# A Mamba layer and a mixture-of-experts block on one core: power, routing, transfers, projection and final sums rearranged

## The chip, the core and the metric

The kernel runs on one core of a Trainium2 chip. Five engines work side by side, each through its own queue in order: TensorE (PE) multiplies matrices into PSUM, VectorE (DVE) does element-wise work, statistics and scans, ScalarE (ACT) applies functions with a scale and a bias, GpSimd (POOL) does small element-wise work and issues the indirect transfers, SyncE (SP) issues most of the plain transfers. The metric is the time of the device in microseconds, as the median of several runs.

## The reference

Two layers over 4 sequences of 1024 tokens with 128 features, in float32.

```python
# layer 1: Mamba, then LayerNorm of x + layer
xb, z = split(x @ in_proj_w.T)                  # 256 channels each
xb = silu(conv4(xb)); dt_in, Bp, Cp = split(xb @ x_proj_w.T)
dt = softplus(dt_in * dt_w + dt_b); A = -exp(A_log)
h[t] = exp(dt*A) * h[t-1] + (xb*dt) * Bp[t]     # 16 states for each channel
y = (h * Cp).sum(states) + xb * D
x = layernorm(x + (norm(y) * ln_g + ln_b) * silu(z) @ out_w.T)
# layer 2: attention, then 16 experts of which each token takes two
hidden = x + causal_attention(norm(x), 16 heads of 8) @ o_w
xt = norm(hidden); logits = xt @ router_w
top1, top2 = two largest of softmax(logits), with a limit of 512 rows per expert
eout[e] = gelu(rows_of_e @ fc1_w[e]) @ fc2_w[e] * 0.8
moe = g1 * eout[top1] + g2 * eout[top2]
x = layernorm(x + hidden + moe)
```

A token's row stands in its expert's list at the count of earlier tokens with the same choice, so routing needs running counts over all tokens.

## The kernel before

The tokens are 32 tiles of 128, a sequence is 8 tiles, a half of a sequence is 4. Everything lies in one program with two branches; the one that runs is the one under `with tc.If(mild > 0)`.

**Stage 1, scans.** `fronts` makes the projections and the convolution. `scans` then takes the halves of the sequences one after the other; the scans proper are VectorE instructions over 512 tokens (L511), with the exponentials from ScalarE (L505) and products on both sides (L501, L517), and the sums over states on TensorE (L521). After the scans of a half, `after_scans` norms y and projects it: it makes y centred on TensorE (`pt_yc`, L449), multiplies it into the gate on VectorE (`sz`) and squares it on ScalarE (`sq`), sums the squares on TensorE into the variances (`pv`, L469), takes their power -0.5, and projects the gated rows (`pa`). `on_half` then norms the rows twice (`lnx`) and `inputs` of the attention makes queries and keys from them (`xh`, `pt_xn`, `pq`), which go out to DRAM (`q_parts`, `k_parts`) and come back spread (`qst`, `kst`).

**Stage 2, attention.** `stream` goes through blocks of 128 keys against 512 queries: scores on TensorE (L742), exponentials on ScalarE (L752), weighted sums on TensorE (L764). When the four groups of heads of a half are done, `rest_of_half` (or `group_of_last` for the very last half) divides, projects, and `after_projection` adds, norms (`hid` to `xrow`, with `normalise_in_pieces`), transposes (`pt_x2`) and makes the router's logits (`lg`).

**The order.** From the second sequence on, TensorE and VectorE run in the order in which the program is written (`manual_schedule`, engines in `pinned`); for the other engines a scheduler chooses. The streams of work are Python generators that `piece` advances in turn: `before` (what leads to the next inputs: `after_scans`, `inputs`), `after` and `final` (what follows attention), `aside` (the routing of tiles that are ready), `loads` (the experts' weights) and `sending` (row transfers). A piece contains one step of the attention (`next(attend)`). A generator that yields `USE` has its next part put ahead of the attention's block, others behind. `pace.first` holds from the end of the scans on: then `before` gets an extra step.

**Routing.** `routing` gives `send(t0, n, later)`: the two largest logits for n tiles, running counts by products with a triangle and with ones on TensorE (`pcum`), the slot of each row (`put`), and then one indirect transfer for each tile and choice (`scatter`, line L126) from `xrow` to the experts' lists `xin` in DRAM. It is called three times, for 20, 8 and 4 tiles. The transfers of the first call carry no group, and so each waits until the one before it has landed; from the second call on they are declared independent of each other.

**Powers.** `inv_std` adds epsilon on VectorE and takes the power on GpSimd, for all norms (L152).

**Stage 3, experts.** For each of 16 experts: rows read from `xin`, transposed, multiplied (`ph`), GELU on ScalarE (`hT`), multiplied (`po_e`), bias added (`eo`), and written by four indirect transfers to `eout`, at the place of the token. `all_sent` computes the final gates after the third expert.

**Final sums.** For each four tiles both choices' rows are read (`got0`, `got1`), multiplied by the gates and added to the residual rows `x1` on VectorE (L1446), normed (`lno`) and written out.

Of the kernel before, what the change touches and what calls it, by code (L numbers as in the profile page):

```python
# [10 lines left out]
F32 = mybir.dt.float32  # L11
BF16 = mybir.dt.bfloat16
I32 = mybir.dt.int32
AF = mybir.ActivationFunctionType
# [5 lines left out]
P = 128  # L20
B, L, D = 4, 1024, 128
T = B * L
# [30 lines left out]
def mamba_then_moe_block_kernel(ctx: ExitStack, tc: tile.TileContext, a: dict, out: bass.AP):  # L53
# [43 lines left out]
    pace = Step(slack=False, hold=False, first=False, block=False, quiet=0)  # L97

    def slack():
        if pace.slack:  # L100
            yield
# [52 lines left out]

    def normalise(*args):
        for _ in normalise_in_pieces(*args):
            pass

    def normalise_in_pieces(pool, src, dst, n, tag):

        mv = statistics(pool, src, n, tag)
        r = inv_std(pool, mv[:, :, 1], n, tag)
        yield USE
        apply_norm(src, dst, mv, r, n)
# [174 lines left out]
    def scans(ph, pools, on_loads, on_scans, on_half, spare_bank=lambda: None):  # L339
# [99 lines left out]
        def after_scans(b, hf, y, sz, r):  # L439
# [26 lines left out]
            pv = bank("pv")  # L466
            for i in range(TPH):
                for c in range(NC2):
                    nc.tensor.matmul(  # L469
                        pv[:, i : i + 1], lhsT=sqs[c][:, i * P : (i + 1) * P], rhs=mean_col,  # L470
                        start=(c == 0), stop=(c == NC2 - 1),
                    )
            yield USE
            rs = inv_std(n2, pv[:, 0:TPH], TPH, "ssm")
            yield
            pa = project("pa", sz, w_out)
            yield from slack()
            yield USE
# [137 lines left out]
    def attention(ph, weights, last_bank):  # L616
# [235 lines left out]
        def group_of_last(e, g, t, rows, i0, n):  # L852
# [28 lines left out]
            if g < NG - 1:  # L881
                yield
# [6 lines left out]
            if g == NG - 1:  # L889
                pace.quiet += 1  # L890
                yield USE
                yield from after_projection(e, po, rows, i0, n, e.hid if i0 else None)

        def tokens_of_half(e, po, rows):
            if pace.first:
                pace.quiet += 1
            poT = p1.tile([P, 512], F32, tag="poT", name="poT")
            nc.scalar.activation(poT, po, AF.Identity, bias=ob)
            yield
            pt = bank_z("pt_po")  # L900
            for i in range(4):
                nc.tensor.transpose(pt[:, i * P : (i + 1) * P], poT[:, i * P : (i + 1) * P], ident)
            yield from slack()
            yield USE
            yield from after_projection(e, pt, rows, 0, TPH)

        def after_projection(e, pt, rows, i0, n, hid=None):
# [18 lines left out]
            if pace.quiet:  # L926
                pace.quiet -= 1
# [238 lines left out]
    def routing(ph, bank):  # L1166
# [51 lines left out]
        def send(t0, n, later=None):  # L1218
# [14 lines left out]

            group = (f"sent{t0}", []) if t0 or later is None else None
            earlier = sent[-1] if sent else []
            if group:
                sent.append(group[1])

            def transfers(i):
                for t in range(t0, t0 + n):  # L1240
                    ins = scatter(xin, put[i][:, t : t + 1], xrow[:, t, :], group, earlier)
                    if group and (len(group[1]) == 1 or earlier):
                        wait_for(ins, earlier)
                    yield
# [70 lines left out]
            if later is not None:  # L1315
                yield
# [67 lines left out]
    def experts(ph, weights, behind, sent, all_sent):  # L1384
# [4 lines left out]
        p4 = ph.enter_context(tc.tile_pool(name="moe4", bufs=4))  # L1389
        ps_t = ph.enter_context(tc.tile_pool(name="ps_t", bufs=2, space=PSUM))  # L1390
# [42 lines left out]


        x1 = p1.tile([P, NT, D], F32, tag="x1", name="x1")
        nc.sync.dma_start(x1, rest_d.rearrange("(i p) d -> p i d", p=P))
        for t0 in range(0, NT, 4):
            s = p3.tile([P, 4, D], F32, tag="s", name="s")
            for k in range(2):
                r = p3.tile([P, 4, D], F32, tag=f"got{k}", name=f"got{k}")  # L1440
                read = (nc.sync, nc.scalar)[k].dma_start(
                    r, eout[k * T + t0 * P : k * T + (t0 + 4) * P, :].rearrange("(i p) d -> p i d", p=P)
                )
                wait_for(read.ins, made[1])
                for i in range(4):
                    nc.vector.scalar_tensor_tensor(  # L1446
                        s[:, i, :], r[:, i, :], gates[k][:, t0 + i : t0 + i + 1],
                        x1[:, t0 + i, :] if k == 0 else s[:, i, :], ALU.mult, ALU.add,
                    )
            o = p3.tile([P, 4, D], F32, tag="o", name="o")  # L1450
            normalise(p3, s, o, 4, "lno")
            nc.sync.dma_start(out[t0 * P : (t0 + 4) * P, :].rearrange("(i p) d -> p i d", p=P), o)
# [6 lines left out]
    with tc.If(mild > 0) as cmp:  # L1459

        with ExitStack() as late:
            with ExitStack() as ph:
# [8 lines left out]
                def piece():  # L1471

                    pace.block = False
                    for at in (USE, None):
                        for s in (late_loads, before, after, final, aside, loads, sending):
                            if at is None:
                                pause = middle and not pace.block
                                if s is after and pace.hold or s is before and pace.first:
                                    continue
                                if s is loads and (before or pause) or s is sending and (pace.quiet or pause):  # L1480
                                    continue
# [75 lines left out]
                xrow, send, all_sent, (behind, sent), rows.tri = routing(late, lambda name: (last_bank if before else bank)(name))  # L1557
# [23 lines left out]
            experts(late, moe_w, behind, sent, lambda: all_sent(early))  # L1581
    with cmp.Else():
# [21 lines left out]
        with ExitStack() as late:  # L1604
# [7 lines left out]
            experts(late, moe_w, behind, sent, lambda: all_sent(NT // 2))  # L1612
# [67 lines left out]
```

## Time and profile before

| | |
|---|---|
| time before, median of 3 runs | 1277.02 us (1276.29 to 1282.18) |
| the profiled execution | 1282.12 us, its span 1280.3 us |
| TensorE busy | 934.2 us, 73% of the span |
| VectorE busy | 890.2 us, 70% |
| ScalarE busy | 644.3 us, 50% |
| GpSimd busy | 247.9 us, 19% |
| mean granted TensorE clock | 0.813 |
| last scan starts | 859.8 us |
| first read of the experts' rows is issued | 1077.1 us |
| first read of the final sums is issued | 1229.1 us |

In lines of the timeline the columns are the start and the duration in us, the engine, the line of the kernel, the operation, the tiles (out<-in) with shapes, the number of instructions merged, and in brackets how long the engine stood idle before and which instruction ended that. In the table of stages each engine's busy time is followed by its number of instructions; PEclk is the granted TensorE clock, 1.0 being full speed. A wait is put down to what came last by the profile. `L` numbers are lines of the kernel before. The profiled execution was at the upper end of the runs.

### The profile page before, as it was taken

The numbers are of one execution on the slowest core, as the hardware profiler recorded it, in microseconds if no ns is written. First come the engines' busy times: TensorE is split into PE (matmuls) and PEld (weight loads), VectorE is DVE, ScalarE is ACT, GpSimd is POOL, SyncE is SP. The second block draws the span as 40 slices with busy tenths as digits, with TensorE's granted clock in tenths as the row PEclk, the third lists the DMA queues.
The fourth block names the chain that finished last, engine by engine and source line by source line (L and its number), as shares of the span: only waits on it lengthen the run. The fifth ranks groups of instructions, "written<-read, shape, count | busy, mean of one in ns | idle before, by whom it ended". The sixth has DMA issues, their size and how long they took to land. (4 is left out here: it accounts for less than half of the span.)

```text
span 1280.3 us, 14950 instructions
## 1 busy us (share of the span) xinstructions
PE 934.2 (73%) x5248; PEld 428.1 (33%) x5248; DVE 890.2 (70%) x1319; ACT 644.3 (50%) x900; POOL 247.9 (19%) x225
## 2 busy tenths in 40 slices
PE   4687851358798988799887599878759863998910
PEld 2232310035333334234333233334313322665610
DVE  2299698998998987988999998896324433212146
ACT  1467556334876775477774278753333621332300
POOL 0020121022102001011003120101232342344421
PEclk9988975557998889689888679889676865999965
DMA  3965576426545433552552441243543115122042
GB/s 72 335 232 174 195 260 230 161 99 193 176 127 167 148 120 121 152 154 91 167 178 90 155 131 38 84 119 84 168 137 96 35 34 184 60 66 65 29 131 84
DMA packets 168311, 170.99 MB, mean 134 GB/s; under 512 B 31537, under 2 KB 123138, under 8 KB 168098
## 3 DMA queue, kind: packets, MB, share of 16 engines
q1 hardware_dynamic: 150818, 142.11, 35.9%
q10 hardware_dynamic: 13312, 19.40, 4.3%
q0 software_dynamic: 4096, 8.43, 1.9%
q8 instruction: 43, 0.70, 0.2%
q14 instruction: 42, 0.34, 0.1%
HBM read 110.80 MB, written 59.10 MB: 133 GB/s over the span
## 5 line engine op out<-in xcount | busy, mean ns | idle before, releaser
L752 ACT ACTIVATE pr<-pst 128x1024 f32<-128x1024 f32 (+3 forms) x396 | 293.2, 792 | 122.8 <-PE pst L742 61.1
L505 ACT ACTIVATE da<-dt_sp,a_neg 128x512 f32<-128x512 f32 x256 | 179.1, 721 | 111.9 <-DVE h L511 101.5
L742 PE MATMUL pst<-qst,kst 72*128 72x512 bf16 (+3 forms) x792 | 205.6, 363 | 36.2 <-ACT pr L752 26.7
L764 PE MATMUL av<-pr,vp 128*32 128x512 f32 (+3 forms) x1584 | 192.4, 554 | 4.5 <-DVE pr L755 2.6
L511 DVE TENSOR_TENSOR_SCAN h<-da,carry,h 128x512 f32<-128x512 f32 x128 | 156.0, 1268 | 1.7 <-ACT da L505 1.7
L501 DVE TENSOR_TENSOR h<-u_sp,bt 128x2048 f32<-128x2048 f32 x64 | 145.4, 2276 | 16.0 <-DMA u_sp<-u_d 16.0
L511 DVE TENSOR_TENSOR_SCAN h<-da,h 128x512 f32<-128x512 f32 x128 | 148.7, 1207 | 6.6 <-ACT da L505 6.6
L517 DVE TENSOR_TENSOR h<-h,ct 128x2048 f32<-128x2048 f32 x64 | 146.3, 2285 | 1.1 <-POOL carry L514 0.3
L521 PE MATMUL py<-h,sel 128*32 128x512 f32 x512 | 87.3, 762 | 81.3 <-DVE h L517 53.7
L742 PEld LDWEIGHTS <-kst 72*128 72x128 bf16 x792 | 68.2, 106 | 186.9 <-issue 170.6
L514 POOL COPY carry<-h 128x4 f32<-128x4 f32 x32 | 40.0, 1249 | 353.1 <-DVE h L511 353.1
L1412 ACT ACTIVATE hT<-ph,b 128x512 f32<-128x512 f32 x64 | 43.9, 687 | 89.4 <-PE ph L1411 87.8
L126 POOL DMA_INDIRECT xin<-xrow,put x64 | 63.6, 994 | 104.5 <-DMA xin<-xrow,put 87.5
L126 POOL DMA_INDIRECT eout<-eo,to x64 | 61.5, 960 | 91.0 <-DVE eo L1423 55.7
L1411 PE MATMUL ph<-xeT,w 128*128 128x512 f32 x128 | 64.3, 639 | 12.9 <-DVE xeT L1407 12.9
L281 PE MATMUL pt_x<-xT,w_tap 128*128 128x512 f32 x128 | 60.6, 629 | 17.5 <-DVE w_tap L263 7.4
L1418 PEld LDWEIGHTS po_e<-w,hT 128*128 128x128 f32 x512 | 61.5, 192 | 13.2 <-issue 12.7
L748 PE MATMUL pst<-mask_k,identb 128*128 128x128 bf16 x448 | 63.9, 227 | 0.0
L1418 PE MATMUL po_e<-w,hT 128*128 128x128 f32 x512 | 63.2, 277 | 0.1
L764 PEld LDWEIGHTS av<-pr,vp 128*32 128x32 f32 x1584 | 36.9, 114 | 65.2 <-issue 39.7
L748 PEld LDWEIGHTS <-identb 128*128 128x128 bf16 x448 | 43.7, 103 | 26.7 <-issue 7.6
L521 PEld LDWEIGHTS py<-h,sel 128*32 128x32 f32 x512 | 12.1, 120 | 120.1 <-DVE h L517 66.8
(231 smaller groups left out, 1098.4 us busy)
## 6 DMA issues: line engine op xcount, KB each, us to landing
dt_sp<-dt_d SPq DMA_DIRECT2D x64, 256.0 KB
u_sp<-u_d SPq DMA_DIRECT2D x64, 256.0 KB
kst<-k_parts SPq DMA_DIRECT2D x96, 144.0 KB
qst<-q_parts SPq DMA_DIRECT2D x64, 144.0 KB
bt<-bc_d SPq DMA_DIRECT2D x32, 256.0 KB
ct<-bc_d SPq DMA_DIRECT2D x32, 256.0 KB
w<-in_fc_w_dram SPq DMA_DIRECT2D x32, 256.0 KB
xin<-clear SPq DMA_DIRECT2D x8, 516.0 KB
```

Source lines behind the costliest of these rows:

```text
L126: ins = nc.gpsimd.indirect_dma_start(out=dst[:, :], out_offset=bass.IndirectOffsetOnAxis(ap=rows, axis=0), in_=src, in_offset=None).ins
L501: nc.vector.tensor_tensor(s.h, s.u, four(s.bt), ALU.mult)
L505: nc.scalar.activation(s.da[jl], s.dt[:, jl, :], AF.Exp, scale=a_neg[:, j, s.g : s.g + 1])
L511: ins = nc.vector.tensor_tensor_scan(h, s.da[jl], h, from_, ALU.mult, ALU.add).ins
L517: nc.vector.tensor_tensor(s.h, s.h, four(s.ct), ALU.mult)
L521: nc.tensor.matmul(s.py[jl * NR : (jl + 1) * NR, :], lhsT=sel, rhs=s.h[:, jl, :], start=(s.g == 0), stop=(s.g == NG_S - 1),)
L742: nc.tensor.matmul(pst[:, jj, :w], lhsT=ks[ki // TPH][jp][:, jj, ki % TPH * P : (ki % TPH + 1) * P], rhs=qs[jp][:, jj, q0:c1], start=True, ...
L748: nc.tensor.matmul(pst[:, jj, :P], lhsT=identb, rhs=mask_k, start=False, stop=True)
L752: nc.scalar.activation(pr[:, :, :w], pst[:, :, :w], AF.Exp, scale=QSCALE)
L764: nc.tensor.matmul(av[32 * j : 32 * j + 32, q0 : q0 + w], lhsT=e.vps[ki // TPH][:, ki % TPH, v0 : v0 + 32], rhs=pr[:, jj, :w], start=(ki = ...
L1411: nc.tensor.matmul(phh, lhsT=w1[e][:, c * P : (c + 1) * P], rhs=xeT, start=True, stop=True)
L1418: nc.tensor.matmul(po[:, i, :], lhsT=hT[:, c, i * P : (i + 1) * P], rhs=w2[e][:, c, :], start=(c == 0), stop=(c == NFC - 1),)
```

## The change

1. *No power on GpSimd without scans*: where `pace.first` holds, `normalise_in_pieces` takes the power by three Newton steps on VectorE, 14 instructions, and no longer yields in between.
2. *Projection with the variances*: where a second PSUM bank is free (`spare_bank`), `after_scans` writes `pv` there and issues `pa` right behind it; the rest of the half before is held meanwhile (`pace.hold`).
3. *Routing behind inputs*: `aside` and the transfers advance only when `before` is empty; transfers and loads only with an attention block. The counter `quiet`, which held transfers off while a power was due, goes. The routing's bank is the common one.
4. *Transfers not in turn*: the first call's transfers get a group too. After the first choice's transfers the routing yields `USE`.
5. *Final sums by TensorE*: each gate is put on a diagonal by ScalarE (`by_gate`), during the experts in the source; two products per tile add both choices in PSUM. The residual rows are read into `xrow` after the third expert. ScalarE norms by scale and bias. Both choices lie in one tile, five deep. The last group is two groups of two tiles.

```diff
+    def inv_std_steps(pool, var, n, tag):
+        ve = pool.tile([P, n], F32, tag=tag + "_ve", name=tag + "_ve")
+        nc.vector.tensor_scalar(ve, var, LN_EPS, None, ALU.add)
+        r = pool.tile([P, n], F32, tag=tag + "_rs", name=tag + "_rs")
+        t = pool.tile([P, n], F32, tag=tag + "_nt", name=tag + "_nt")
+        nc.vector.tensor_scalar(r.bitcast(I32), ve.bitcast(I32), 1, None, ALU.logical_shift_right)
+        nc.vector.tensor_scalar(r.bitcast(I32), r.bitcast(I32), -1.0, float(0x5F3759DF), ALU.mult, ALU.add)
+        for _ in range(3):
+            nc.vector.tensor_tensor(t, r, r, ALU.mult)
+            nc.vector.tensor_tensor(t, t, ve, ALU.mult)
+            nc.vector.tensor_scalar(t, t, -0.5, 1.5, ALU.mult, ALU.add)
+            nc.vector.tensor_tensor(r, r, t, ALU.mult)
+        return r
...
-        r = inv_std(pool, mv[:, :, 1], n, tag)
-        yield USE
+        if pace.first:
+            r = inv_std_steps(pool, mv[:, :, 1], n, tag)
+        else:
+            r = inv_std(pool, mv[:, :, 1], n, tag)
+            yield USE
...
-            pv = bank("pv")
+            other = spare_bank()
+            pv = (other or bank)("pv")
...
+            if other:
+                pace.hold = True
+                pa = project("pa", sz, w_out)
+                yield from slack()
             yield USE
             rs = inv_std(n2, pv[:, 0:TPH], TPH, "ssm")
-            yield
-            pa = project("pa", sz, w_out)
-            yield from slack()
-            yield USE
+            pace.hold = False
+            if other:
+                yield USE
+            else:
+                yield
+                pa = project("pa", sz, w_out)
+                yield from slack()
+                yield USE
...
-            if g < NG - 1:
+            if not i0:
                 yield
             po = zbank("po") if i0 else e.po
...
-            group = (f"sent{t0}", []) if t0 or later is None else None
+            group = (f"sent{t0}", [])
             earlier = sent[-1] if sent else []
-            if group:
-                sent.append(group[1])
+            sent.append(group[1])
...
             if later is not None:
-                yield
+                yield USE
...
+                nc.sync.dma_start(xrow[:, :, 0:D], rest_d.rearrange("(i p) d -> p i d", p=P))
+                by_gate = p6.tile([P, NT, 2, P], F32, tag="by_gate", name="by_gate")
+            elif e > 2:
+                per = -(-NT // (E - 3))
+                for t in range((e - 3) * per, min((e - 2) * per, NT)):
+                    for k in range(2):
+                        nc.scalar.activation(
+                            by_gate[:, t, k, :], ident, AF.Identity, scale=gates[k][:, t : t + 1]
+                        )
...
-        x1 = p1.tile([P, NT, D], F32, tag="x1", name="x1")
-        nc.sync.dma_start(x1, rest_d.rearrange("(i p) d -> p i d", p=P))
...
-                    nc.vector.scalar_tensor_tensor(
-                        s[:, i, :], r[:, i, :], gates[k][:, t0 + i : t0 + i + 1],
-                        x1[:, t0 + i, :] if k == 0 else s[:, i, :], ALU.mult, ALU.add,
...
+        for t0, n in [(t, 4) for t in range(0, NT - 4, 4)] + [(NT - 4, 2), (NT - 2, 2)]:
+            both = ps_h.tile([P, CAP], F32, tag="ph", name="both")
+            for i in range(n):
+                for k in range(2):
+                    nc.tensor.matmul(
+                        both[:, i * D : (i + 1) * D], lhsT=by_gate[:, t0 + i, k, :], rhs=gots[t0 + i][:, k, :],
+                        start=(k == 0), stop=(k == 1),
+                    )
+            s = p3.tile([P, 4, D], F32, tag="s", name="s")[:, :n, :]
+            nc.vector.tensor_tensor(
+                s, both[:, : n * D].rearrange("p (i d) -> p i d", d=D), xrow[:, t0 : t0 + n, 0:D], ALU.add
+            )
+            mv = statistics(p3, s, n, f"lno{n}")
+            nm = p3.tile([P, 4], F32, tag="lno_nm", name="lno_nm")[:, :n]
+            nc.vector.tensor_scalar(nm, mv[:, :, 0], -1.0, None, ALU.mult)
+            r = inv_std(p3, mv[:, :, 1], n, f"lno{n}")
+            sh = p3.tile([P, 4], F32, tag="lno_sh", name="lno_sh")[:, :n]
+            nc.gpsimd.tensor_tensor(sh, nm, r, ALU.mult)
+            o = p3.tile([P, 4, D], F32, tag="o", name="o")[:, :n, :]
+            for i in range(n):
+                nc.scalar.activation(
+                    o[:, i, :], s[:, i, :], AF.Identity, bias=sh[:, i : i + 1], scale=r[:, i : i + 1]
+                )
...
-                                pause = middle and not pace.block
                                 if s is after and pace.hold or s is before and pace.first:
                                     continue
-                                if s is loads and (before or pause) or s is sending and (pace.quiet or pause):
+
+                                if s is aside and before or (s is loads or s is sending) and (before or middle and not pace.block):
                                     continue
...
-                xrow, send, all_sent, (behind, sent), rows.tri = routing(late, lambda name: (last_bank if before else bank)(name))
+                xrow, send, all_sent, (behind, sent), rows.tri = routing(late, bank)
```

## The prediction

> **What bounds the kernel now.** I first read the table of stages (busy time of each engine in stretches of the span), because this program runs through four stages with different limits, then the waits of VectorE, then the timeline around the two longest stalls, and last the chain that ended last.
>
> ```profile
> core 0: us, PE busy (x) PEld busy (x) DVE busy (x) ACT busy (x) POOL busy (x), PEclk, DMA share, GB/s
> 300.00:400.00 100.00, 87.76 (x651) 41.97 (x653) 87.86 (x109) 69.99 (x104) 15.13 (x8) 0.95 0.50 158
> 950.00:1000.00 50.00, 40.22 (x178) 13.56 (x182) 18.02 (x58) 17.06 (x23) 17.29 (x18) 0.58 0.23 71
> 1240.00:1280.30 40.30, 0.00 (x0) 0.00 (x0) 28.27 (x139) 0.00 (x0) 7.12 (x7) 0.50 0.37 103
> ```
>
> With scans (to about 862 us) VectorE and TensorE are both at 88%. Without scans (862 to 1060) VectorE is at 36%, and TensorE, at a granted clock of 0.58, carries the time. In the last 40 us TensorE and ScalarE do nothing and VectorE runs alone with GpSimd.
>
> The waits of VectorE with scans, 100 to 862 us (total, times, longest):
>
> ```profile
> DVE ssm_ve L150 <- PE pv L469: 13.6, 7, 3.5
> DVE xh L176 <- POOL lnx_rs L490: 9.2, 6, 1.5
> DVE x L480 <- PE pa L425: 2.6, 3, 1.1
> ```
>
> Seven times VectorE stands still for the variances of the centred rows, 1.9 us each.
>
> The timeline without scans, for the longest stall:
>
> ```profile
> 944.21 0.17 DVE L150 TENSOR_SCALAR ln_ve<-ln_mv 128x4 f32<-128x4 f32 x1
> 956.44 1.07 POOL L152 TENSOR_TENSOR ln_rs<-ln_ve,neg_half 128x4 f32<-128x4 f32 x1
> 957.94 1.25 PE L936 MATMUL pt_x<-ident,xrow 128*128 128x128 f32 x4 [10.39 <-DVE xrow L176]
> ```
>
> The variance is ready at 944.4, but its power starts at 956.4: GpSimd's queue stood in row transfers, each waiting for the one before it. The list of all waits has POOL xin behind DMA xin at 87.5 us in 41 waits. TensorE was idle for 10.39 us.
>
> The inputs of the last half of a sequence, TensorE's lines of the same timeline:
>
> ```profile
> 893.86 1.38 PE L645 MATMUL pt_xn<-ident,xh 128*128 128x128 f32 x4 [5.15 <-DVE xh L176]
> 907.57 2.07 PE L661 MATMUL pq<-xnT,wk 128*128 128x512 f32 x2 [2.61 <-DVE rest L667]
> 915.83 1.01 PE L742 MATMUL pst<-qst,kst 72*128 72x512 bf16 x2 [2.51 <-DMA qst<-q_parts]
> ```
>
> From the last y at 865.8 to the first score at 915.83 it takes 50 us, with TensorE waiting on VectorE, which meanwhile routes 20 token tiles.
>
> The chain that ended last, in the final sums:
>
> ```profile
> 1263.71 1.11 DVE o L176 x4
> 1264.83 1.31 DVE s L1446 x5
> 1266.14 0.40 DVE lno_st L170 x2
> 1267.13 0.24 DVE s L1446
> 1267.92 1.02 POOL lno_rs L152
> ```
>
> One group of four tiles every 5.25 us, on VectorE, with a wait of 0.94 us for the power.
>
> **What the Trainium skill says.** (1) "TensorE: Matmul & The Clock Gate", section "HAM oscillation — how this bites in real kernels", warns of idle gaps over about 3.4 us, after which TensorE's clock halves. The trace agrees as to the fall (clock 0.50 from 945 to 982) but not as to recovery: from 958 TensorE was busy, and it stayed at 0.50 until about 982. (2) "DMA: Bandwidth & Descriptors", section "Anatomy of one DMA — SWDGE (gpsimd) path", gives a nearly fixed 2 us, most of it the receipt of the write. Here 0.96 us of issue and at least 1.6 us of wait: 2.5 us and more for each transfer in turn, against 1.27 us start to start where they don't wait (1023 to 1036). (3) "SBUF — State Buffer", section "Who interferes with whom", has GpSimd and VectorE block each other on a shared port pair. The power of 128x4 took 1.01 us while VectorE was quiet and 1.85 to 3.00 among scans.
>
> **The change, part by part.** The sum is made on the profiled execution: span 1280.3, 1.8 us around it, 1282.1.
>
> Final sums. Removed from VectorE: per group 8 multiply-adds (8 x 0.26 us start to start) and 4 normalisations (1.11 us). There remain one add from PSUM (0.69, the row of eo, same shape), statistics of 4 tiles (1.16, the 1.40 of the trace less the 0.24 of a multiply-add between them) and two small ones (0.24): 2.1 us; for seven groups of four and two of two some 17.2 us. TensorE gets 64 products, two passes each: 128 x 0.12 us (26 passes of po_e took 3.1), at half clock 0.215 (eight passes of ph took 6.62 against 3.70). The first 6.6 us of the experts after idling were at half clock, so I take 7 us for two groups, then 95 x 0.12 = 11.4: 18.4 us, beside VectorE. ScalarE takes the four normalisations, some 0.31 us each (row probs, 128x128), 1.2 us a group: hidden. GpSimd gets a second small product per group, which no row shows quiet: between 0.3 and 1.25 us (the carry copy among scans); I take 0.6, so 2.2 us a group with the hand-overs, just about VectorE's pace. Transfers: 4 MB in and 2 MB out at the 300 GB/s seen at 1231 to 1235 need 21 us, also about that pace. First data 1233.5 (as now, k=1), first sums 1236.9, VectorE done 1254.1, then power, product and normalisation of two tiles (1.9) and the 5.3 us from the last row to the end as now: 1261.3. The gain is 19 us; 10.7 if TensorE stays at half clock (128 x 0.215 = 27.5), 12.8 if GpSimd sets 2.8 us a group, 21 at best. The read of the residual rows (2 MB, now at 1060.7 in the wait for the last transfers) moves into the third expert, on SP ahead of the fourth expert's rows; there the queue sat waiting for buffers, so nothing.
>
> Gates on diagonals: 64 ScalarE instructions. In the order of the changed program 30 stand ahead of the first GELU. The gates are ready at 1070.1, 30 x 0.31 = 9.3 us end at 1079.4, and the table load before the first GELU came at 1084.18: hidden. 14 follow the first expert (4.3 us in the 5.9 us of idle ahead of the second): hidden. Of 20 around the second expert's GELUs, 6 us, the third expert's GELUs (1103.1) are late by some 3: I charge 2.5, with ends 0 and 6.
>
> Power on VectorE without scans: 14 dependent steps of 128x4 or 128x2 at 0.21 us (the routing's steps of 128x20 follow each other so, 889.5 to 890.4) are 2.9 us, in place of 1.0 on GpSimd. At the stall: from the transposed projection 0.15 + 0.72 + 1.73 + 0.12 + 2.9 + 0.33 = 6.0 us to the first row, less 2 to 3 us of TensorE work between: TensorE waits 3.7 in place of 10.4, and its wait of 2.2 us just before (on a masked tile behind those statistics) goes: gain 8.5. The last norm lies on the path: 1.9 more. The one before it meets a projection put one block later, which saves some of the 3.41 us TensorE waited at 1033.45 and adds as much at the transposes: nothing. Together 2 lost.
>
> Routing behind inputs: VectorE has the centred rows before the first routing steps. The projection pa follows pv at once (876.5 against 882.8), lnx_rs ends 881.4 (887.7), xh comes at 881.5 (893.47), but TensorE's po of 5.4 us and blocks of scores now stand ahead of pt_xn: about 887 against 893.9; then pt_x waits for 14 steps and the q projection follows at 894 (901.5), k at 902 (907.6). First score 908.3 against 915.8: 7.5 gained (6 to 9). The routing's 80 products of ones move into attention, where TensorE is the bound: 3.2 us twice at half clock less some, 5 lost.
>
> Transfers not in turn: 40 at 1.27 us in place of about 130 us. GpSimd has no other work on the path then, since the power left; what they cost is bounded below.
>
> Projection with the variances, with scans: VectorE reads pv after another pair of scans (2.4 us), which covers most of the seven waits of 1.9. The power (1.9 us) hides behind one 2.28 us product. Up to 12 gained, none if ScalarE's or TensorE's blocks take the waits over, as TensorE is at 88% too: I take 7.
>
> Sum: -7 -7.5 +5 -8.5 +2 +2.5 -19 = -32.5; the profiled execution would be 1249.6. The median of the runs is 5.1 below it (1277.0), so 1244.5; I say 1244.
>
> **Rivals.** *The clock stays up.* The routing's full-width products come early in the last half's attention and the idle of 10 us goes; of the 46 us that TensorE works at 0.50 from 917 to 998 about a third could fall away: 15 more, 1229. For it: the clock rose at 900 and at 983, each time in such products. Against: the remaining wait of 3.7 us. *Little from the scans, a slow tail.* The seven waits only move (7 less) and TensorE stays at half clock to the end (8.3 less): 1260. *Transfers back to back hold the others up.* While GpSimd issued back to back (1022.8 to 1036.9, 14.1 us), TensorE waited 3.41 and 3.15 us for VectorE and ScalarE, which stood 6.4, 5.5 and 5.1 us on a releaser the profile calls remote: 47% of that time. In the change 56 transfers, 71 us, are back to back during attention. At 47% that is 33 less the 6.6 paid already, 27 lost: 1271, no change. From 64% on (32.5 + 6.4 + 6.6 of 71) the kernel is slower; at 80% it gives 1294. Against it: eight in a row at 1065 to 1075 showed nothing, though nothing waited there. *No effect*: were the powers not taken off GpSimd, the middle would stay; in the changed order they are off it.
>
> **How the numbers follow.** 0.5%, 6.4 us, is about what a measurement of this kernel can tell from no change. Chances: the forecast 0.60 (1232 to 1257), clock up 0.18, slow tail 0.14, hold-up at 1271 0.04, slower at 1294 0.04. Faster by over 0.5%: 0.92; within: 0.04; slower: 0.04. The range takes half of the clock's case and the slow tail: 1223 to 1262.
>
> **What would show it.** Final stage some 32 us from the first read to the end, VectorE 2.1 us a group; no power on GpSimd from 880 until the final sums; TensorE's wait at pt_x under 4 us; first score of the last half near 908; ssm_ve waits under 3 us in all; the third expert's GELU late by 3 us or less. It is wrong if a longer wait stands at the transposes, if remote waits grow with the transfers, or if the scan stage ends later than 862.

## The result and the profile after

The changed kernel takes 1285.62 us (median of 20 runs, 1274.61 to 1292.38) beside 1276.62 us for the kernel before: a ratio of 1.0069, with a 95% interval of 1.0041 to 1.0097. It is 9 us slower, where 33 less were forecast. The profiled execution has a span of 1289.3 us at a mean clock of 0.822. Medians and ranges in this document are over all runs of a kernel; ratios and their intervals leave out runs in a slower state that some executions fall into.

The same program, run again later beside the kernel before, took 1234.58 us (4 runs, 1227.79 to 1240.49), a ratio of 0.968 (0.964 to 0.9716). The record names the chip of this later run, but not that of the first measurement. Both times are measured; why they differ is what this section and the next are about. I call the second one "the changed kernel again".

Marks in the three traces (start of the instruction, us):

| | before | changed | changed again |
|---|---|---|---|
| last `y` of the scans | 865.1 | 854.6 | 846.3 |
| first row transfer | 890.8 | 904.8 | 894.3 |
| 40th row transfer | 1015.8 | 955.8 | 945.5 |
| read of rows for the first expert | 1077.1 | 1102.1 | 1040.3 |
| first read of the final sums | 1229.1 | 1255.4 | 1192.9 |
| end | 1280.3 | 1289.3 | 1226.0 |

From the first transfer to the first expert's rows the changed kernel takes 197.3 us in the one trace and 146.0 in the other: 51.3 us apart. From there to the end the two agree to 1.5 us. Of the 63.3 us between the two spans, 8.3 lie ahead of the last `y` and 2.2 between it and the first transfer. So most of the time is lost while GpSimd sends rows.

The table of stages for those transfers, in steps of 20 us; the columns are the stretch, its length, then for each engine busy us and instructions, the clock, the DMA share and GB/s. The changed kernel first:

```profile
core 0: us, PE busy (x) PEld busy (x) DVE busy (x) ACT busy (x) POOL busy (x), PEclk, DMA share, GB/s
905.00:925.00 20.00, 10.33 (x77) 3.39 (x76) 7.27 (x23) 4.19 (x5) 14.21 (x15) 0.71 0.53 167
925.00:945.00 20.00, 4.00 (x13) 0.69 (x13) 1.72 (x5) 2.15 (x3) 15.12 (x17) 0.50 0.16 53
945.00:965.00 20.00, 2.43 (x13) 0.66 (x12) 2.40 (x6) 2.72 (x4) 8.99 (x10) 0.50 0.10 34
```

The changed kernel again, from the same point of the program:

```profile
894.50:914.50 20.00, 16.11 (x104) 4.98 (x103) 12.04 (x34) 8.73 (x12) 14.24 (x15) 0.79 0.55 167
914.50:934.50 20.00, 15.46 (x64) 6.63 (x63) 7.52 (x33) 6.77 (x10) 15.12 (x17) 0.76 0.58 172
934.50:954.50 20.00, 19.99 (x91) 5.80 (x90) 8.30 (x20) 8.37 (x12) 9.25 (x10) 0.60 0.26 77
```

GpSimd does the same in both (15, 17 and 10 instructions). In the first trace the other engines do little beside it: TensorE is busy for 16.8 of 60 us, in the second for 51.6.

Whom they wait for, in the list of all waits of the changed kernel from 905 to 965 us (total, times, longest):

```profile
PE pr L868 <- DVE avs L870: 34.5, 2, 21.4
ACT pr L780 <- PE pr L868: 24.9, 1, 24.9
DVE avs L870 <- remote: 23.0, 1, 23.0
ACT pr L780 <- remote: 22.1, 3, 15.3
```

"remote" is what the profile writes where it finds no releaser. Read the chain backwards: TensorE waits for VectorE's `avs`, and VectorE and ScalarE wait for something out of sight. The timeline of the changed kernel shows what they were due after (start, duration, engine, instruction, idle before it):

```profile
916.37 1.03 PE L770 MATMUL pst<-qst,kst 72*128 72x512 bf16 x2 [4.49 <-issue]
917.57 1.04 PE L770 MATMUL pst<-qst,kst 72*128 72x512 bf16 x2 [0.16 <-issue]
...
931.36 1.02 ACT L780 ACTIVATE pr<-pst 128x1024 f32<-128x1024 f32 x1 [15.30 <-remote]
...
933.56 0.58 PE L868 MATMUL pr<-ih,sel_b 48*128 48x512 bf16 x1 [13.10 <-DVE avs L870]
...
936.26 1.02 ACT L780 ACTIVATE pr<-pst 128x1024 f32<-128x1024 f32 x1 [3.77 <-PE pst L770]
...
960.71 0.69 DVE L870 TENSOR_TENSOR avs<-avs,pr 128x512 f32<-128x512 f32 x1 [22.97 <-remote]
```

The exponentials of 931.36 and 936.26 belong to the scores of 916.37 and 917.57: 15.0 and 18.7 us from start to start. The multiplication at 960.71 needs the product of 933.56: 27.2 us. The changed kernel again has the same pairs so:

```profile
903.79 0.61 PE L770 MATMUL pst<-qst,kst 72*128 72x512 bf16 x2 [2.46 <-DMA kst<-k_parts]
904.50 1.02 ACT L780 ACTIVATE pr<-pst 128x1024 f32<-128x1024 f32 x1 [2.88 <-PE pst L770]
905.26 0.61 PE L770 MATMUL pst<-qst,kst 72*128 72x512 bf16 x2 [0.86 <-DMA kst<-k_parts]
...
905.96 1.02 ACT L780 ACTIVATE pr<-pst 128x1024 f32<-128x1024 f32 x1 [0.34 <-PE pst L770]
907.48 0.60 PE L868 MATMUL pr<-ih,sel_b 48*128 48x512 bf16 x1
...
908.12 0.69 DVE L870 TENSOR_TENSOR avs<-avs,pr 128x512 f32<-128x512 f32 x1 [0.68 <-PE pr L868]
```

There it is 0.7, 0.7 and 0.6 us. In the first trace's semaphore records the update that frees the exponential of 931.36 stands at 931.27, for products whose modelled end is 917.4. What comes from the other engines is on time: VectorE's `avs` ended at 933.51 and TensorE started at 933.56. So in these pairs the others learn late that TensorE is done, while a result of VectorE is seen at once. As the ends of products are modelled, the trace doesn't tell whether the products or only their signals were late.

The final sums, for which the prediction took 19 us off. The last 40 us in the table of stages of the changed kernel:

```profile
1249.00:1289.30 40.30, 17.08 (x128) 16.88 (x128) 16.23 (x92) 13.29 (x32) 14.06 (x22) 0.74 0.62 166
```

And some lines of its timeline near the end:

```profile
1277.71 1.01 POOL L152 TENSOR_TENSOR lno_rs<-lno_ve,neg_half 128x4 f32<-128x4 f32 x1 [0.84 <-DVE lno_ve L150]
1278.59 0.42 DVE L1486 TENSOR_TENSOR s<-both,xrow 128x256 f32<-128x256 f32 x1 [0.22 <-ACT o L1497]
1278.80 0.20 POOL L1494 TENSOR_TENSOR lno_sh<-lno_nm,lno_rs 128x4 f32<-128x4 f32 x1
1279.03 1.65 ACT L1497 ACTIVATE o<-s,lno_sh,lno_rs 128x128 f32<-128x128 f32 x4 [0.48 <-DVE s L1486]
1279.62 1.01 POOL L152 TENSOR_TENSOR lno_rs<-lno_ve,neg_half 128x4 f32<-128x4 f32 x1 [0.62 <-DVE lno_ve L150]
```

TensorE, VectorE, ScalarE and GpSimd now share the last 40 us, where VectorE was busy for 28.27 of them with only GpSimd beside it. Here one group of four tiles follows the other after 1.9 us (1277.71 to 1279.62, from power to power); over the seven groups of four it is 2.1 us on average, instead of 5.25. From the first read to the end it takes 33.9 us instead of 51.2.

The scans: VectorE's waits with scans, 100 to 854 us, the changed kernel:

```profile
DVE xh L195 <- POOL lnx_rs L518: 6.1, 4, 1.5
DVE sz_s L476 <- PE pt_yc L468: 5.6, 3, 2.7
DVE x L508 <- POOL ssm_rs L152: 4.8, 5, 1.0
DVE x L508 <- PE pa L444: 2.5, 2, 1.3
```

The 13.6 us of `ssm_ve` behind `pv` have gone from the head of the list; a new wait for the power (4.8) is smaller.

### The profile page after: what moved, and what is told of

The parts are those of the page before. It is cut to its first block, busy times and chain, and to the rows that moved or that the text cites. A ratio compares the mean times of both kernels' runs of the same rounds, so it can differ in the third digit from the quotient of the medians.

```text
span 1289.3 us, 15308 instructions
## 1 busy us (share of the span) xinstructions
PE 937.8 (73%) x5376; PEld 445.8 (35%) x5376; DVE 879.9 (68%) x1298; ACT 673.6 (52%) x996; POOL 240.3 (19%) x231
## 5 line engine op out<-in xcount | busy, mean ns | idle before, releaser
L770 PE MATMUL pst<-qst,kst 72*128 72x512 bf16 (+3 forms) x792 | 199.2, 353 | 50.6 <-ACT pr L780 32.7
L792 PE MATMUL av<-pr,vp 128*32 128x512 f32 (+3 forms) x1584 | 186.9, 542 | 2.4 <-DVE pr L783 1.9
L529 DVE TENSOR_TENSOR h<-u_sp,bt 128x2048 f32<-128x2048 f32 x64 | 145.3, 2274 | 17.1 <-DMA sz_d<-sz 17.1
L300 PE MATMUL pt_x<-xT,w_tap 128*128 128x512 f32 x128 | 62.8, 649 | 16.8 <-DMA xT<-in_xT_dram 7.5
L1441 PE MATMUL po_e<-w,hT 128*128 128x128 f32 x512 | 63.3, 276 | 0.1
```

The source lines that it names most:

```text
L529: nc.vector.tensor_tensor(s.h, s.u, four(s.bt), ALU.mult)
L770: nc.tensor.matmul(pst[:, jj, :w], lhsT=ks[ki // TPH][jp][:, jj, ki % TPH * P : (ki % TPH + 1) * P], rhs=qs[jp][:, jj, q0:c1], start=True, ...
L792: nc.tensor.matmul(av[32 * j : 32 * j + 32, q0 : q0 + w], lhsT=e.vps[ki // TPH][:, ki % TPH, v0 : v0 + 32], rhs=pr[:, jj, :w], start=(ki = ...
L1441: nc.tensor.matmul(po[:, i, :], lhsT=hT[:, c, i * P : (i + 1) * P], rhs=w2[e][:, c, :], start=(c == 0), stop=(c == NFC - 1),)
```

## The experiments

Two theories stood at first. **H, hold-up:** the third rival; row transfers without a pause between them hold up the others. **O, order:** the new order of the routing and the powers costs the time, whatever the transfers do. Each group of kernels below ran on one chip, beside the kernel before; the groups fell on five different chips, none of which came twice.

### First group: the transfers

`in_turn`, the changed kernel with the condition of before:

```diff
-            group = (f"sent{t0}", [])
+            group = (f"sent{t0}", []) if t0 or later is None else None
             earlier = sent[-1] if sent else []
-            sent.append(group[1])
+            if group:
+                sent.append(group[1])
...
-                    if len(group[1]) == 1 or earlier:
+                    if group and (len(group[1]) == 1 or earlier):
```

> The changed kernel with one part undone: the 40 row transfers of the first 20 tiles again each wait for the one before it. Theory H (hold-up): while GpSimd issues transfers without a pause, what TensorE has finished is seen late by the other engines, and that costs about 35 us between 905 and 960. Then this kernel is near 1250 us (1243 to 1260), the 40 transfers take some 130 us instead of 50, and no wait put down to 'remote' is longer than 5 us. Theory O (order): the loss comes from the new order of the routing and of the powers, whatever the transfers do. Then it stays at 1280 to 1290.

Measured: 1243.54 us, ratio 0.975 (0.9708 to 0.9793). The waits of its stage without scans hold

```profile
POOL xin L126 <- DMA xin<-xrow,put: 80.5, 41, 5.6
...
DVE loc L1199 <- remote: 8.7, 1, 8.7
```

GpSimd stands in its transfers for 80.5 us, and nobody minds; the one "remote" wait falls on the second call's 16 transfers, which are still back to back (1011 to 1029). It was longer than the 5 us I allowed. H holds.

`before_free`, the kernel before with the opposite of that diff:

> The kernel before with this one part of the change alone: the 40 transfers no longer wait for each other. H: it is slower than the kernel before by 15 to 35 us (1292 to 1312), with waits put down to 'remote' of 10 us and more during the 50 us of transfers; what it saves at the stall of 10 us at the transposes, where the power stood behind the transfers, may give back up to 10 of it. O: it is as fast as before or faster by up to 10 us (1267 to 1277).

Measured: 1296.55 us, ratio 1.0172 (1.0119 to 1.0226), with "remote" waits of up to 23.5 us. The transfers alone make the kernel before slower; O falls.

`twice` adds, after each of the 40 transfers, one into a tensor that nothing reads:

```diff
+                    if not earlier:
+                        scatter(copy, put[i][:, t : t + 1], xrow[:, t, :], more)
```

> The changed kernel with each of the 40 transfers followed by a second one of the same rows into a tensor that nothing reads (80 transfers without a pause, about 101 us instead of 50). H: the hold-up lasts twice as long, 30 to 45 us more, 1315 to 1330. O: 1280 to 1290 as in the changed kernel, since nothing waits for the second rows.

Measured: 1336.72 us, ratio 1.0463 (1.0407 to 1.0518): 51 us above the changed kernel, and above the 1315 to 1330 that I expected. The table of stages of `twice`, at the end of the 80 transfers:

```profile
950.00:1000.00 50.00, 3.19 (x13) 0.66 (x12) 1.54 (x3) 1.62 (x2) 38.11 (x40) 0.50 0.16 53
```

In those 50 us GpSimd issues 40 transfers and no other engine is busy for more than 3.2 us. The DMA engines are busy for 16%: it isn't their bandwidth.

`two_ahead` was meant to let each transfer wait for the second one before it:

```diff
-            wait_for(ins, first)
+            wait_for(ins, first if earlier else group[1][-2:][:1])
```

> The changed kernel, but each of the 40 transfers waits for the one two before it (two in flight at most). If H is a matter of GpSimd issuing without a pause, the pauses help in proportion: some 65 to 75 us for the 40 transfers, and 1250 to 1265. If two transfers in flight are enough for the hold-up, it stays near 1285, as it does under O.

Measured: 1291.6 us, ratio 1.0102 (1.004 to 1.0163). The edit doesn't do what was meant. In the trace the third, fourth and fifth transfers wait for nothing, and from the tenth on the waits are those of the changed kernel: each transfer waits for the semaphore that it uses itself, which the eighth one before it used. None waits for the second one before it, and the 40 transfers still start 1.26 us apart. So the run says nothing of two in flight. It is in effect the changed kernel once more, on the chip of this group: 1291.6 us, beside 1243.5 with the transfers in turn.

### Second group: pauses, plain transfers, the sums alone

`pause_short` puts a small GpSimd instruction between two transfers of the first two calls; `pause_long` two memsets of 512 columns:

```diff
+                    if later is not None:
+                        for after_this in rested:
+                            in_order(ins, after_this)
+                        still = nc.gpsimd.memset(rest_tile[:, 0:1], 0.0).ins
+                        in_order(still, ins)
+                        rested[:] = [still]
```

> The changed kernel with a GpSimd memset of one column (0.10 us elsewhere in its trace) after each transfer of all groups but the last: GpSimd still never waits, and a transfer starts every 1.4 to 1.7 us. Theory W (waiting): other engines see TensorE's completion signals only when GpSimd stands still in a wait. Then the hold-up stays: 1285 to 1305. Theory C (continuous DMA issue): what holds the signals is one DMA issue directly behind another, and any other instruction between two lets them through. Then it is 1235 to 1250, below the kernel with transfers in turn, as the second group of transfers starts earlier.

> As the kernel with the short memset, with two memsets of 512 columns (about 0.5 us each): a transfer every 2.4 to 2.9 us, the pace of the transfers in turn, but GpSimd always busy. W: the hold-up stays and lasts twice as long, 1310 or more. C: no hold-up, 1240 to 1255, as with the transfers in turn. A third theory, R (rate), that only the number of transfers in a stretch counts: also 1240 to 1255, while the short memset then leaves 1270 to 1290.

Measured: 1232.17 us (ratio 0.9681, 0.9655 to 0.9707) and 1231.39 us (0.9676, 0.9647 to 0.9704), with no "remote" wait in either. It looked like theory C. But the transfers of `pause_short` started 1.26 us apart as before, since the memset fits into the gap of 0.30 us that each issue leaves (those of `pause_long` 2.25 us apart), and the next groups overturned the reading.

`plain` has plain transfers in place of those by row numbers. As its condition asks for an empty list of earlier ones, all 64 became plain, not the first 40 alone: no rows reach the experts' lists.

> The changed kernel with the first group's 40 transfers made plain ones from GpSimd's queue (the rows go in order to a tensor that nothing reads, so the rows of the first 20 tiles are left out of the experts' inputs): no row numbers, the same bytes. If the hold-up comes with the addressing by row numbers, it goes: 1240 to 1255. If any DMA that GpSimd issues without a pause does it, there are again waits put down to 'remote' of 10 us and more, and 1275 to 1295.

Measured: 1217.32 us, ratio 0.9549 (0.9512 to 0.9586), no "remote" wait. They started before the row numbers were there, and the experts no longer waited for the last of them, so the time says little about the hold-up.

`sums_only`, the kernel before with the new `experts`:

> The kernel before with the last part of the change alone: gates on diagonals, final sums by TensorE, the rest rows read during the third expert. The prediction's terms for it are 19 us gained and 2.5 lost: ratio 0.987, some 1257 us beside 1273.6. The rival of a slow tail gives 0.993; no gain would say that the sums were not on the path.

Measured: 1257.91 us, ratio 0.9879 (0.9854 to 0.9904): 15.4 us less by the ratio, 17.3 by the medians. The two terms, -19 and +2.5, came out to within about 1 us together.

### Third group: single parts

`scan_only` is the kernel before with the change's hunk in `after_scans` alone; `turn_pow` and `turn_early` are `in_turn` with

```diff
-        if pace.first:
+        if False:
             r = inv_std_steps(pool, mv[:, :, 1], n, tag)
```

and with

```diff
-                                if s is aside and before or (s is loads or s is sending) and (before or middle and not pace.block):
+                                if (s is loads or s is sending) and (before or middle and not pace.block):
```

> The kernel before with one part of the change alone: with scans the out projection follows the variances at once. The prediction took 7 us for it, with ends 0 and 12: 1268 beside 1275, ratio 0.9945. In the changed kernel the last y of the scans came at 854.6 instead of 865.1, so if that is this part's doing it should show 10 us here, ratio 0.992; if it is owed to something else in the change, 1.000.

Measured: 1259.27 us, ratio 0.9883 (0.9848 to 0.9919): 15 us, twice the 7 that I took. Its last `y` stands at 845.3.

> The kernel with the transfers in turn, with the powers of the stage without scans back on GpSimd. The prediction's terms say the powers on VectorE gain 8.5 at the stall and lose 2 at the end: this kernel is then 6.5 us slower than with the transfers in turn, 1250 (ratio 0.980), with a wait of some 10 us of TensorE at pt_x. If the stall came only of the old order, no wait longer than 5 us and 1241 to 1244.

> The kernel with the transfers in turn, with the routing no longer held behind the inputs of the last half. The prediction's terms (7.5 gained with the inputs, 5 lost in attention) make it 2.5 us slower than with the transfers in turn, 1246 (ratio 0.977); 1236 to 1241 if the earlier transfers end earlier and that counts more, since in the kernel with transfers in turn the last of them ends 27 us after the last token is ready.

Measured: `turn_pow` 1251.54 us (six runs, 1231.33 to 1254.18; the ratio, 0.9717 with 0.9651 to 0.9782, rests on two of them, 1231.33 and 1245.42) and `turn_early` 1237.76 us (0.9707, 0.9666 to 0.9749). Both intervals overlap that of `in_turn` (0.9708 to 0.9793), which ran on another chip: neither the powers' nor the routing's share of the time is shown. The wait at `pt_x` that `turn_pow` was to bring back did come, 9.8 us in its trace.

`plain_late` repeats `plain` with 80 plain transfers that wait for the row numbers (the rows of the first 20 tiles don't reach the experts):

> The changed kernel with plain transfers (no row numbers) from GpSimd's queue in place of the first group's 40, each twice into tensors that nothing reads and none before the row numbers are there: 80 issues of 0.53 us, 42 us without a pause in the same place. The rows of the first 20 tiles are left out of the experts' inputs. If the hold-up comes of the transfers by row numbers alone: no wait put down to 'remote' longer than 2 us in that stretch, and below 1240. If any DMA issue on GpSimd directly behind another does it: such waits of 10 us and more, and 1265 to 1290.

Measured: 1236.06 us, ratio 0.9694 (0.9645 to 0.9742), no "remote" wait. But neither had `scan_only` one during its own 15 transfers back to back (1000.0 to 1018.7), where the kernel before had three of 5 to 6 us in its trace. Nothing was held up on this chip, so plain transfers aren't cleared by it.

### Fourth group: the memset falls as the cure

> The changed kernel with the memset of one column after every 4th transfer only. If signals held back are let through at each memset, a hold-up lasts 5 us at most: waits put down to 'remote' of under 5 us, and 1232 to 1245. If four in a row are too few to hold anything up (as in the experts' stage, where transfers go in fours), none, and 1229 to 1235. If a memset is needed after each one, 1270 or more.

> As with every 4th, but after every 10th (12.6 us of transfers in a row). If the memset lets the held signals through: waits put down to 'remote' of up to 12 us, some 10 to 20 us lost in all, 1242 to 1255. If the hold-up grows without end once it has begun, as in the changed kernel: 1270 or more.

> The kernel before with the transfers not in turn (1296 without a memset), and the memset after each. If the memset alone takes the hold-up away whatever the order of the work, no wait put down to 'remote' over 2 us and 1262 to 1278: as the kernel before or some us faster, since the power at the transposes stands behind fewer transfers. If the hold-up in this order has another cause, 1290 and more.

> The changed kernel with the memset after each transfer (1232), and the routing not held behind the inputs of the last half. The prediction's terms (7.5 gained by holding it back, 5 paid in attention) make it 2.5 us slower, 1235; if the earlier routing takes work out of the end, as with the transfers in turn (0.9707 against 0.975), some 4 us faster, 1228.

`pause_4` and `pause_10` are `pause_short` with

```diff
-                        still = nc.gpsimd.memset(rest_tile[:, 0:1], 0.0).ins
+                        for _ in range(len(group[1]) % 4 == 0):
+                            still = nc.gpsimd.memset(rest_tile[:, 0:1], 0.0).ins
```

(10 for 4); `free_pause` has the diff of `pause_short` in `before_free`, and `early_pause` that of `turn_early` in `pause_short`. Measured: 1280.41 us (ratio 1.0021, 0.9996 to 1.0045), 1280.16 us (1.0021, 0.9997 to 1.0045), 1297.53 us (1.0101, 1.0033 to 1.0168) and 1287.76 us (1.0061, 1.003 to 1.0093), and the longest "remote" wait between 17.9 and 27.7 us. The timeline of `early_pause`, which has a memset after every transfer:

```profile
908.46 0.12 POOL L1278 MEMSET rest_tile<- 128x1 f32 x1
908.77 0.95 POOL L126 DMA_INDIRECT xin<-xrow,put  x1 [0.19 <-issue]
909.72 0.12 POOL L1278 MEMSET rest_tile<- 128x1 f32 x1
909.90 0.69 ACT L698 ACTIVATE hi<-pq,kb 128x512 bf16<-128x512 f32 x1 [4.25 <-remote]
```

ScalarE waits 4.25 us for a product of TensorE with a memset in every gap. The memset doesn't prevent the hold-up.

### Fifth group: the memset or the chip

The changed kernel, unchanged, and `pause_short` once more, on one chip:

> The changed kernel itself, beside the one with a memset after each transfer, on one chip. If the memset takes the hold-up away: 1275 to 1292 here, with waits put down to 'remote' of 10 us and more, and 1229 to 1235 there. If the chip decides and this is one that holds up: 1275 to 1292 in both. If the chip decides and this is one that does not: 1228 to 1245 in both, no such wait, and the records of the transfers' semaphores complete (256 for each of eight), as on the two chips without a hold-up.

> The changed kernel with the memset of one column after each transfer, once more (1232 before). Memset decides: 1229 to 1235 while the changed kernel beside it is at 1275 or more. Chip decides: within 10 us of the changed kernel beside it, either both at 1275 to 1292 or both at 1228 to 1245.

Measured: 1234.58 us (0.968, 0.964 to 0.9716) and 1229.93 us (0.962, 0.9591 to 0.965), no "remote" wait in either. So it isn't the memset that decides, but something that goes with the group: its chip, or the time of its runs. The two can't be told apart here, as no chip came twice.

| group | kernels | "remote" waits during the transfers |
|---|---|---|
| first measurement, chip not on record | before, changed | yes |
| first | `in_turn`, `before_free`, `twice`, `two_ahead` | yes |
| second | `pause_short`, `pause_long`, `plain`, `sums_only` | no |
| third | `scan_only`, `turn_pow`, `turn_early`, `plain_late` | no |
| fourth | `pause_4`, `pause_10`, `free_pause`, `early_pause` | yes |
| fifth | `after_again`, `pause_again` | no |

The sides differ in one more thing: the trace of the changed kernel holds 937 semaphore records of GpSimd's transfers, the one of the same program again 2058, with 15,308 instructions in both. All twenty traces divide so: at most 1575 such records where there are "remote" waits, at least 2056 where there are none. Of TensorE's own records some are missing too (1537 against 1569). Whether the missing records and the late signals are one thing, or what sets the groups apart, isn't settled. One rival was not tested at all: every run on record was recorded with its span and clock, so nothing tells whether the hold-up is there in a run that isn't recorded. Nor is it shown in what way the kernel before escapes: its median lies between 1273.6 and 1277.6 us in every group, though 5 us of hold-up might be expected to show. And where transfers are held up, only waiting for each one was tried: whether a slower pace without waiting (`pause_long`) or plain transfers would help there stays open, since both ran where nothing was held up.

## Why the prediction was wrong

**The failed step** is "Transfers not in turn: 40 at 1.27 us in place of about 130 us. GpSimd has no other work on the path then", which charged nothing, and the chance of 0.08 for the rival that it named. The rival's mechanism was right, its place was right, and so was its formula. Measured, 51.3 of the 71 us of transfers are held up, 72%; its limit was 64%. With its own terms, -32.5 + 51.3 - 6.6 = +12 us; measured +9. That the sum comes so near is in part luck: where nothing was held up the change gained 41 us, not 32.5, and the 6.6 for the kernel before don't show in its medians. What was weak is the evidence against it: "eight in a row at 1065 to 1075 showed nothing, though nothing waited there" can't speak against a hold-up, as the sentence says itself. The three waits in the trace for it, 47% of the only burst that anyone waited in, deserved the larger share:

```profile
1031.11 1.76 DVE L878 RECIPROCAL rd_all<-pr 128x256 f32<-128x256 f32 x1 [6.39 <-remote]
1038.93 0.42 DVE L915 TENSOR_TENSOR hid<-po,x 128x256 f32<-128x256 f32 x1 [5.54 <-remote]
1039.03 1.08 ACT L752 ACTIVATE pr<-pst 128x512 f32<-128x512 f32 x2 [5.12 <-remote]
```

Where nothing was held up the time fell into the range (1234.6 in 1223 to 1262), 9 us below the 1244 forecast. Of the signs of being wrong that it named, "remote" waits grew with the transfers, and TensorE's wait at `pt_x` was not under 4 us. The other terms were off both ways:

**Scans, -7.** Right in kind, too small: 15 us (`scan_only`), beyond the end of 12. Of the 13.6 us of waits on `ssm_ve` 2.0 are left (1.6 again); I took half back for other engines, and they took little.

**Inputs of the last half, -7.5.** From the last `y` to the first score it took 50.8 us, then 42.4 (changed) and 40.2 (again): 8.4 and 10.6 gained. As times of the trace, the first score came at 897.0, not 908, since the scans ended 10.5 us earlier. That the routing's place is worth the 5 us lost elsewhere isn't shown (`turn_early`).

**Stall at pt_x, -8.5.** At the stall the wait fell from 10.39 to 4.4 us (4.5 again), near the 3.7 worked out. But TensorE's waits at the transposes of all four parts, in total, times and longest, up to 1060 us, for the kernel before, the changed kernel again and `turn_pow`, are

```profile
PE pt_x L936 <- DVE xrow L176: 13.3, 2, 10.4
PE pt_x L959 <- DVE xrow L195: 16.5, 4, 4.9
PE pt_x L959 <- DVE xrow L195: 13.3, 3, 9.8
```

The steps on VectorE make four waits of 3.3 to 4.9 us out of one long and one short, 3 us more in all. The 2 us lost at the last norm came as worked out (2.9 to 4.9). Of the two new waits the prediction has one in its term for the inputs; the other it set off against a wait elsewhere. What the powers bring to the time isn't shown (`turn_pow`).

**Experts, +2.5.** From the first expert's rows to the first read of the final sums: 152.0 us before, 153.3 after, 152.6 again: about 1 us.

**Final sums, -19.** 17.3 (18.1 again); VectorE and TensorE as worked out, 16.2 and 17.1 us busy against 17.2 and 18.4.

**Where the rest lies.** Without a hold-up the stage from the last `y` to the experts' rows is 18 us shorter (212.0 to 194.0); the terms say -7.5 + 5 - 8.5 + 2 = -9. Some 5 to 7 of the rest may have been the kernel before's own hold-up: in `sums_only` and `scan_only`, which leave that stage's code as it was and were not held up, it took 207.5 and 204.9. I had counted them in the rival only. As the medians of the kernel before don't differ between the groups, this isn't shown.

**Readings of the trace that were wrong.** VectorE's 36% and the clock of 0.58 are those of 950 to 1000; over 862 to 1060 the trace has 41% and 0.72. And it doesn't agree with the warning on idle gaps as to the fall of the clock: it fell at 944.6 us, ahead of the gap of 10.39 us (947.6 to 957.9), after a gap of 2.23:

```profile
944.75 0.98 PE L764 MATMUL av<-pr,vp 128*32 128x128 f32 x8 [2.23 <-DVE pr L755]
945.67 1.89 PE L742 MATMUL pst<-qst,kst 72*128 72x512 bf16 x4
```

So this trace gave no ground to count on a higher clock once that gap went. Of the powers among scans, two (381.3 and 487.3 us) took 1.01 us and not 1.85 to 3.00.

The Trainium skill's page "DMA: Bandwidth & Descriptors" (Anatomy of one DMA — SWDGE (gpsimd) path), which I named for the price of transfers in turn, was no guide to the cost of transfers that aren't: it speaks of the transfer's own latency, and the cost lay with engines that have nothing to do with it.

## What to carry to other kernels

A wait between transfers on GpSimd may be what keeps the others running: before you remove it, look at what the other engines do in the bursts that the profile already has, and give a hold-up seen there the weight of its measured share. Where transfers are held up, those in turn (1243.5 us) are the version to keep; elsewhere the changed kernel is within 5 us of the fastest that was run with the same work, and one with transfers in turn (`turn_early`, 0.9707 against 0.968) hardly slower. And run the unchanged program beside a supposed cure, on the same chip, before you name it one: four kernels seemed to be cured by a pause or by plain transfers, and had only run where nothing is held up. Last, look in the trace whether a wait that you wrote is there: that of `two_ahead` wasn't.

## What the runs showed of the hardware that was not expected

- In three of six sets of runs, while GpSimd issued indirect transfers 1.26 us apart, other engines took up TensorE's results late: 15.0, 18.7 and 27.2 us after the start of the products in the changed kernel's trace, against 0.6 to 0.7 where nothing was held up. A result of VectorE was taken up within 0.05 us meanwhile. In the same sets no such wait was seen while the transfers waited for each other, 2.5 us and more apart (`in_turn`).
- The same program took 1285.6 us in one set of runs and 1234.6 in another, while the kernel before took 1276.6 and 1276.7 beside it.
- A GpSimd memset of one column (0.12 us) between two transfers took no time of its own: they still started 1.26 us apart.
